# An LSTM with a sign-weight FFN on one core: Wx in two pieces, twelve steps' x products ahead, and FFN weights made from step 4

## The chip, the core and the metric

The kernel runs on one NeuronCore of a Trainium2 chip. The time is that of the device for one execution, in microseconds (us); the kernel before has three such runs. A profiled execution, taken by the hardware profiler, is a fourth one: its trace gives every duration below.

Five engines work beside each other, each with its own queue of instructions: TensorE (PE: matrix products; its weight loads are the row PEld), VectorE (DVE), ScalarE (ACT), GpSimd (POOL) and SyncE (SP, which here only issues DMA requests). ACT and POOL issue DMA requests too. Matrix products accumulate in PSUM; everything else lies in SBUF, 128 partitions wide.

## What is computed

The input x has N=32 sequences of T=64 steps with D=256 features. An LSTM with H=256 runs over it, and its outputs go through three layers whose weights are boolean matrices read as +1 and -1:

```python
def lstm_forward(x, h0, Wx, Wh, b):
    xW = jnp.einsum('ntd,dg->ntg', x, Wx) + b
    def step(carry, xw_t):
        prev_h, prev_c = carry
        a = xw_t + prev_h @ Wh            # 4 gates of 256
        i, f, o = sigmoid(a[:, :Hd]), sigmoid(a[:, Hd:2*Hd]), sigmoid(a[:, 2*Hd:3*Hd])
        g = jnp.tanh(a[:, 3*Hd:])
        next_c = f * prev_c + i * g
        next_h = o * jnp.tanh(next_c)
        return ((next_h, next_c), next_h)
...
h = jnp.concatenate([hs, -hs], axis=-1)
h = relu(s0 * conn_dense(k0, h)) * 2      # 512 -> 1024, conn_dense: w = where(k, 1.0, -1.0)
h = relu(s1 * conn_dense(k1, h)) * 2      # 1024 -> 1024
out = x + s2 * conn_dense(k2, h)          # 1024 -> 256
```

The 64 steps of the LSTM depend on each other; the products of x with Wx and the FFN don't depend on the next step.

## The kernel before

**Layout.** The four quarters (`NQ = 4`) of the 256 features lie in the four groups of 32 partitions; in a product each quarter is a matmul of its own with 32 columns of weights. A product in full f32 is two matmul instructions in the trace. The gates lie in the order of `GATES`: slot 0 is the candidate (tanh), slots 1 and 2 are the sigmoid gates i and f, slot 3 is o.

**Loads (L116-139, L143-146, L430-433).** SP and ACT issue them in the order of the program: the first four steps of x, slots 2 and 3 of Wx (128 KB a request, four requests), x of steps 4 to 7, slots 0 and 1 of Wx, x of steps 8 to 15, then Wh (slot 0, then slots 1 to 3). From there SP alone goes on: x of steps 16 to 31 (L138, L139), the eight requests for k0 (L146), four rows of k1 (L182), x of steps 32 to 47 (L433). ACT has an activation of its own between its requests (L120), which brings in its table of functions. POOL loads the bias, the first h and the scales. The tile framework gives these requests a set of semaphores in turn, so a later request waits until an earlier one has landed.

**Before step 0 (L422-450).** PE runs two matmuls on zeros into the gate banks and `WARM_UP` = 9 more into an idle bank. Then come the products of x with Wx for steps 0 to 7: first slots 2 and 3 of all eight steps (for each step both contraction chunks k), then slots 0 and 1, and after each pair of steps `evict_x` (L238), in which DVE adds the bias and moves two steps to SBUF as `xg`. `x_products(8, AHEAD)` with `AHEAD` = 10 does steps 8 and 9 with all four slots. `turn_x` (L210) is the DVE transpose of half a block of x (eight steps) that these products read.

**The steps (L467-482).** In step t the program issues, in this order:

- `gates_from_h` (L265): 32 matmul instructions, h times Wh, on top of what lies in the two gate banks;
- `cell_step` (L283): on ACT two sigmoids and a tanh, on DVE `kept`, `new`, `c`, on ACT `th`, on DVE `h` and its transpose into `hist`; then ACT copies `xg` of the next step into the gate banks (L280, L281);
- one **chore** from a list of 16, one a step from step 0 on (L458-461, L470): four pieces of w0 (`make_w0`, L186: an ACT instruction on the spot, L189, and a DVE one later in the step, L190), eight rows of w1 (`make_w1`, L194: one ACT instruction of 1024 columns, and the load of another row), four pieces of w2 (`make_w2`, L198);
- work for PE: in steps 0 to 20 (`X_STEPS` = 21) a 21st of the x products that are left, after that a share of the FFN (`ffn_block`, L365). In units of `x_part` (L222; 8 matmul instructions, one step and one chunk of all slots) that is five units in most steps and six in three;
- the DVE half of a w0 chore, and every fourth step `split_h` (L308), which makes the FFN's two-part input (`hhi` on ACT, `hlo` on DVE).

After each pair of steps, `x_products` calls `evict_x`; where the half block after is to be turned (L253-257), it calls `turn_x` and asks for the half block four further on.

After step 63 the last FFN block runs by itself (L484).

Of the kernel before, what the change touches and what calls it, by code (L numbers as in the profile page):

```python
# [32 lines left out]
AF = mybir.ActivationFunctionType  # L33
# [5 lines left out]
def lstm_ffn(ctx: ExitStack, tc: tile.TileContext, x, cond, wx_d, wh_d, b_d, k0_d, k1_d, k2_d, s0_d, s1_d, s2_d, out):  # L39
    nc = tc.nc  # L40
    P = 128
    N, T, D = x.shape
    H = cond.shape[1]
# [6 lines left out]
    SB = 16  # L50
    NB = T // SB
# [2 lines left out]

    GATES = (3, 0, 1, 2)

    AHEAD = 10
    X_STEPS = 21
    WARM_UP = 9

    const = ctx.enter_context(tc.tile_pool(name="const", bufs=1))
    xpool = ctx.enter_context(tc.tile_pool(name="x", bufs=4))
# [10 lines left out]
    def act(shape, dtype, name):  # L73
        return apool.tile(shape, dtype, tag="act", name=name)
# [4 lines left out]
    def load_x(i, half, engines, part=slice(0, SB // 2)):  # L79
        if part.start == 0:  # L80
            xq[i, half] = xpool.tile([P, SB // 2, HQ], F32, tag="x", name=f"x{i}_{half}")
        t0 = i * SB + half * (SB // 2)
        for q in range(NQ):
            engines[q % len(engines)].dma_start(  # L84
                out=xq[i, half][q * N : (q + 1) * N, part],
                in_=x[:, t0 + part.start : t0 + part.stop, ts(q, HQ)],
            )
# [6 lines left out]
    wx = const.tile([P, 2, G], F32, name="wx")  # L94
# [4 lines left out]
    warm = const.tile([P, 40], F32, name="warm")  # L99
# [4 lines left out]
    def rows(t, q):  # L104
        return t[q * 32 : (q + 1) * 32]

    def load_gates(t, w_d, slots, engines):

        w_rows = w_d.rearrange("(q b j) g -> q j b g", q=NQ, b=2)
        s0, n, g0 = slots[0], len(slots), GATES[slots[0]]  # L110
        for q in range(NQ):
            engines[q % len(engines)].dma_start(
                out=rows(t, q)[:, :, s0 * H : (s0 + n) * H], in_=w_rows[q, :, :, g0 * H : (g0 + n) * H]
            )

    load_x(0, 0, [nc.sync, nc.scalar], slice(0, SB // 4))  # L116
    load_gates(wx, wx_d, (2, 3), [nc.sync, nc.scalar])
    load_x(0, 0, [nc.sync, nc.scalar], slice(SB // 4, SB // 2))

    nc.scalar.activation(warm[:, 1:2], warm[:, :1], AF.Sigmoid)  # L120

    b_rows = b_d.rearrange("(g q j) -> q g j", g=4, q=NQ)
    for q in range(NQ):
# [2 lines left out]
    for slot in range(2):  # L126
        load_gates(wx, wx_d, (slot,), [nc.sync, nc.scalar])
    load_x(0, 1, [nc.sync, nc.scalar])
    load_gates(wh, wh_d, (0,), [nc.sync, nc.scalar])
    load_gates(wh, wh_d, (1, 2, 3), [nc.sync, nc.scalar])  # L130
    h_first = const.tile([P, HQ], F32, name="h_first")
    nc.gpsimd.dma_start(out=h_first, in_=cond.rearrange("n (q j) -> q n j", q=NQ))
    scales = []
# [9 lines left out]
    for i in range(2):  # L143
        t = act([P, 2, F0], U8, f"k0_{i}")
# [65 lines left out]
    def turn_x(i, half, part=slice(0, SB // 2)):  # L210
        if part.start == 0:
            xT[i, half] = act([P, SB // 2, 2, N], F32, f"xT{i}_{half}")
        nc.vector.transpose(
            xT[i, half][:, part].rearrange("p t b n -> p (t b n)"),
            xq[i, half][:, part].rearrange("p t j -> p (t j)"),
        )
# [5 lines left out]
    def x_part(p, t, k, slots, start):  # L222

        i, s = divmod(t, SB // 2)
        for q in range(NQ):
            nc.tensor.matmul(  # L226
                p[q * N : (q + 1) * N, t % 2, slots],
                xT[i // 2, i % 2][:, s, k, :],
                wx_q[:, k, q, slots],
                start=start,  # L230
                stop=False,
                skip_group_check=True,
            )

    def x_bank(t):
        return ps_f.tile([P, 2, 4, HQ], F32, tag="pf", name=f"px{t}")

    def evict_x(p, t):  # L238
        xg[t] = gpool.tile([P, 2, 4 * HQ], F32, tag="xg", name=f"xg{t}")
        b = bias[:, :4].rearrange("p g j -> p (g j)").unsqueeze(1).to_broadcast([P, 2, 4 * HQ])  # L240
        nc.vector.tensor_tensor(xg[t], p.rearrange("p t g j -> p t (g j)"), b, ALU.add)  # L241

    def x_products(t0, t1):

        for t in range(t0, t1, 2):
            p = x_bank(t)
            for s in range(2):
                for k in range(2):
                    x_part(p, t + s, k, slice(0, 4), s == 0 and k == 0)
                    if s == 1 and k == 1:  # L250
                        evict_x(p, t)

                        half, left = divmod(t + 2, SB // 2)  # L253
                        if left == SB // 4 and half + 1 < 2 * NB:
                            turn_x(*divmod(half + 1, 2))
                            if half + 5 < 2 * NB:
                                load_x(*divmod(half + 5, 2), [nc.sync])
                    yield 2


# [4 lines left out]
    def gates_from_h(t, hT):  # L265
        for g, slots in zip(gates, (slice(0, 3), slice(3, 4))):
            for k in range(2):
                for q in range(NQ):
                    nc.tensor.matmul(  # L269
                        g[q * N : (q + 1) * N],  # L270
                        hT[:, k, :],
                        wh_q[:, k, q, slots],
                        start=False,
                        stop=(k == 1),
                        skip_group_check=True,
                    )
# [6 lines left out]
    def cell_step(t, c):  # L283
        sig = cell.tile([P, 3, HQ], F32, tag="sig", name=f"sig{t}")
        cand = cell.tile([P, HQ], F32, tag="cand", name=f"cand{t}")
        nc.scalar.activation(sig[:, 0:2, :], gates[0][:, 1:3], AF.Sigmoid)  # L286
        nc.scalar.activation(cand, gates[0][:, 0], AF.Tanh)  # L287
        nc.scalar.activation(sig[:, 2, :], gates[1][:, 0], AF.Sigmoid)  # L288
        kept = cell.tile([P, HQ], F32, tag="kept", name=f"kept{t}")
        nc.vector.tensor_mul(kept, sig[:, 1, :], c)  # L290
        new = cell.tile([P, HQ], F32, tag="new", name=f"new{t}")
        nc.vector.tensor_mul(new, sig[:, 0, :], cand)  # L292
        c = cell.tile([P, HQ], F32, tag="c", name=f"c{t}")
        nc.vector.tensor_add(c, kept, new)  # L294
        th = cell.tile([P, HQ], F32, tag="th", name=f"th{t}")
        nc.scalar.activation(th, c, AF.Tanh)  # L296
        h = cell.tile([P, HQ], F32, tag="h", name=f"h{t}")
        nc.vector.tensor_mul(h, sig[:, 2, :], th)  # L298
        i, s = divmod(t, SH)
        if s == 0:  # L300
            hist[i] = hpool.tile([P, 2, SH * N], F32, tag="hist", name=f"hist{i}")
        hT = hist[i][:, :, ts(s, N)]
        nc.vector.transpose(hT, h.rearrange("p (b j) -> p b j", b=2))  # L303
        if t + 1 < T:
            gates_from_x(t + 1)
        return c, hT
# [116 lines left out]
    for g in gates:  # L423
        g = g.rearrange("p g j -> p (g j)")
        nc.tensor.matmul(g, idle[:, :P], idle[:, : g.shape[1]], start=True, stop=True)
    for n in range(WARM_UP):
        nc.tensor.matmul(p_idle, idle[:, :P], idle, start=True, stop=True)
# [8 lines left out]
    nc.vector.memset(c, 0.0)  # L436

    banks = [x_bank(t) for t in range(0, SB // 2, 2)]
    for slots in (slice(2, 4), slice(0, 2)):
        for t in range(SB // 2):  # L440
            for k in range(2):
                x_part(banks[t // 2], t, k, slots, slots.start == 2 and t % 2 == 0 and k == 0)
            if slots.start == 0 and t % 2:
                evict_x(banks[t // 2], t - 1)
            if slots.start == 0 and t == 1:
                turn_x(0, 1)
    nc.vector.transpose(hT, h_first.rearrange("p (b j) -> p b j", b=2))
    for _ in x_products(SB // 2, AHEAD):
        pass
# [3 lines left out]
    def ffn():  # L453
        for b in range(NB):
            yield from ffn_block(b)


    chores = deque()  # L458
    chores += [lambda k=k, h=h: make_w0(k, h) for k in range(2) for h in range(2)]
    chores += [lambda k=k: make_w1(k) for k in range(FC0)]  # L460
    chores += [lambda k=k, m=m: make_w2(k, m) for k in range(2) for m in range(2)]

    work = x_products(AHEAD, T)
    total_x = (T - AHEAD) * 4
    total_ffn = (NB - 1) * (4 * FC0 + 2 * FC0 * FC1 + 4 * FC1)
    done = 0
    for t in range(T):  # L467
        gates_from_h(t, hT)
        c, hT = cell_step(t, c)
        later = chores.popleft()() if chores else None  # L470
        if outputs and next(outputs[0], "end") == "end":
            outputs.popleft()
        if t == X_STEPS:
            work, done = ffn(), 0
        goal = (t + 1) * total_x // X_STEPS if t < X_STEPS else (t + 1 - X_STEPS) * total_ffn // (T - X_STEPS)
        while done < goal:
            done += next(work)
        if t == X_STEPS - 1:
            next(work, None)
        if callable(later):  # L480
            later()
        if t % SH == SH - 1:
            split_h(t // SH)
# [31 lines left out]
```

## Time and profile before

| What | Value |
|---|---|
| Three runs | 323.43, 323.81, 324.02 us; median 323.81 us |
| Profiled execution, its own time | 325.26 us |
| Its span, first to last instruction | 323.5 us |
| PE busy with matmuls | 309.4 us (96% of the span) |
| DVE, ACT, POOL busy | 154.0, 131.0, 9.2 us |
| Mean granted TensorE clock | 0.991 |
| First product of x | 6.85 us |
| First matmul of step 0, of step 21 | 17.57 us, 89.48 us |

Times in the trace count from the start of the span. In lists of instructions the columns are start, duration, engine, line, operation, output and inputs, how often, and in brackets the idle time just before it on its engine with what ended it. Rows of merged instructions give the stretch from the first one's start to the last one's end. A busy PE is one with matmuls in flight, which need not mean that it runs at its full rate.

### The profile page before, as it was taken

The page shows a single profiled execution, that of the slowest core. Times are in us where ns is not written, and L with a number is a line of the kernel's source. Part 1 is how long each engine was busy: PE and PEld are TensorE (multiplying, and loading weights), DVE is VectorE, ACT ScalarE, POOL GpSimd, SP SyncE. Part 2 cuts the span into 40 slices and gives each one's busy share as a digit, 9 for nine tenths or more (in the row PEclk, how much of TensorE's full clock was granted, in tenths as well). Part 3 has the DMA queues.
Part 4 walks back from the last instruction along what each step waited for, and adds up shares of the span by engine and source line. Part 5 has one row for each costly group of instructions (what it writes and reads, how often), then busy time and mean ns, then how long its engine had stood idle before and what let it go on. Part 6 is the DMA issues. An engine that isn't in the chain of part 4 may idle for free.

```text
span 323.5 us, 9433 instructions
## 1 busy us (share of the span) xinstructions
PE 309.4 (96%) x3979; PEld 236.8 (73%) x3979; DVE 154.0 (48%) x473; ACT 131.0 (41%) x484; POOL 9.2 (3%) x28
## 2 busy tenths in 40 slices
PE   6994999999999999999999999999999999999992
PEld 3963677787777777777777777777777777888881
DVE  1345765767576433334855433457453333811113
ACT  1015578754455434334735333455433432511111
POOL 3500000000000000000000000000000000000001
PEclk9997999999999999999999999999999999999998
DMA  6745321311000000000010100000310000230002
GB/s 147 208 101 149 71 57 35 86 34 35 6 2 2 0 2 2 1 2 2 0 35 2 32 3 2 2 0 9 92 32 4 2 0 2 58 72 2 0 0 65
DMA packets 30937, 10.99 MB, mean 34 GB/s; under 512 B 28008, under 2 KB 30312, under 8 KB 30896
## 3 DMA queue, kind: packets, MB, share of 16 engines
q1 hardware_dynamic: 27616, 8.66, 11.1%
q10 hardware_dynamic: 3008, 1.57, 1.9%
q8 instruction: 31, 0.51, 0.7%
q0 software_dynamic: 272, 0.17, 0.3%
q14 instruction: 10, 0.08, 0.1%
HBM read 8.29 MB, written 2.10 MB: 32 GB/s over the span
## 4 chain that ended last, share of the span: by engine, by line
PE 87%; DMA 5%; DVE 3%; SPq 3%; issue 1%; ACT 1%; DVEq 0%; ACTq 0%
PE p L399 38%; PE gates L269 19%; PE px L226 12%; PE p L371 10%; PE po L384 9%; DMA x<-in_x_dram 2%; DMA wh<-in_L_cond_Wh_dram 2%; SPq L146 1%; SPq L84 1%; DMA k<-in_L_ffn_k_dram 1%; DMA wx<-in_L_cond_Wx_dram 1%; DVE w L190 0%; DVE xg L241 0%; ACT th L296 0%; DVE hist L303 0%
## 5 line engine op out<-in xcount | busy, mean ns | idle before, releaser
L269 PEld LDWEIGHTS gates<-wh,hist 128*32 128x32 f32 x2016 | 54.6, 110 | 30.3 <-issue 14.1
L269 PE MATMUL gates<-wh,hist 128*32 128x192 f32 x2016 | 68.9, 277 | 5.0 <-DVE hist L303 5.0
L226 PE MATMUL px<-wx,xT 128*32 128x256 f32 (+1 forms) x1152 | 62.2, 366 | 1.4 <-DMA wx<-in_L_cond_Wx_dram 1.4
L226 PEld LDWEIGHTS px<-wx,xT 128*32 128x32 f32 x1152 | 41.3, 115 | 13.8 <-issue 2.7
L286 ACT ACTIVATE sig<-gates 128x128 f32<-128x128 f32 x64 | 17.7, 277 | 82.7 <-PE gates L269 82.5
L290 DVE TENSOR_TENSOR kept<-sig,c 128x64 f32<-128x64 f32 x63 | 14.1, 224 | 61.1 <-ACT sig L286 60.9
L296 ACT ACTIVATE th<-c 128x64 f32<-128x64 f32 x64 | 16.4, 257 | 32.0 <-DVE c L294 32.0
L371 PE MATMUL p<-hhi,w 128*128 128x512 f32 x64 | 25.5, 399 | 0.0
L371 PE MATMUL p<-hlo,w 128*128 128x512 f32 x64 | 25.3, 395 | 0.0
L298 DVE TENSOR_TENSOR h<-sig,th 128x64 f32<-128x64 f32 x64 | 14.4, 226 | 20.7 <-ACT th L296 20.7
L241 DVE TENSOR_TENSOR xg<-px,bias 128x512 f32<-128x512 f32 x32 | 21.2, 666 | 5.9 <-POOL nsgn L158 4.8
L280 ACT COPY gates<-xg 128x192 f32<-128x192 f32 x64 | 20.0, 313 | 8.4 <-DVE xg L241 8.4
L303 DVE STREAM_TRANSPOSE hist<-h 128x64 f32<-128x64 f32 x64 | 15.7, 245 | 2.4
L294 DVE TENSOR_TENSOR c<-kept,new 128x64 f32<-128x64 f32 x64 | 14.4, 225 | 2.2
L288 ACT ACTIVATE sig<-gates 128x64 f32<-128x64 f32 x64 | 14.8, 231 | 0.0
L371 PEld LDWEIGHTS p<-hhi,w 128*128 128x128 f32 x64 | 12.0, 188 | 2.8
L287 ACT ACTIVATE cand<-gates 128x64 f32<-128x64 f32 x64 | 14.0, 218 | 0.1
L292 DVE TENSOR_TENSOR new<-sig,cand 128x64 f32<-128x64 f32 x64 | 13.9, 218 | 0.0
L371 PEld LDWEIGHTS p<-hlo,w 128*128 128x128 f32 x64 | 12.0, 188 | 2.6
L399 PE MATMUL p<-a_7h,w 128*128 128x512 f32 x32 | 13.0, 407 | 0.0
L281 ACT COPY gates<-xg 128x64 f32<-128x64 f32 x64 | 13.0, 203 | 0.0
L399 PE MATMUL p<-a_2l,w 128*128 128x512 f32 x32 | 12.9, 403 | 0.0
(121 smaller groups left out, 500.5 us busy)
## 6 DMA issues: line engine op xcount, KB each, us to landing
x<-in_x_dram SPq DMA_DIRECT2D x58, 64.0 KB, 2.4
out_dram<-o SPq DMA_DIRECT2D x28, 64.0 KB, 1.8
bits<-in_L_ffn_k_dram SPq DMA_DIRECT2D x10, 128.0 KB, 2.5
k<-in_L_ffn_k_dram SPq DMA_DIRECT2D x8, 64.0 KB, 2.0
wh<-in_L_cond_Wh_dram SPq DMA_DIRECT2D x2, 192.0 KB, 5.3
wh<-in_L_cond_Wh_dram ACTq DMA_DIRECT2D x2, 192.0 KB, 5.1
wx<-in_L_cond_Wx_dram SPq DMA_DIRECT2D x2, 128.0 KB, 3.5
wx<-in_L_cond_Wx_dram ACTq DMA_DIRECT2D x2, 128.0 KB, 4.1
```

The lines of the kernel that those rows point to most:

```text
L226: nc.tensor.matmul(p[q * N : (q + 1) * N, t % 2, slots], xT[i // 2, i % 2][:, s, k, :], wx_q[:, k, q, slots], start=start, stop=False, ski ...
L241: nc.vector.tensor_tensor(xg[t], p.rearrange("p t g j -> p t (g j)"), b, ALU.add)
L269: nc.tensor.matmul(g[q * N : (q + 1) * N], hT[:, k, :], wh_q[:, k, q, slots], start=False, stop=(k == 1), skip_group_check=True,)
L280: nc.scalar.copy(gates[0], x_t[:, :3])
L286: nc.scalar.activation(sig[:, 0:2, :], gates[0][:, 1:3], AF.Sigmoid)
L288: nc.scalar.activation(sig[:, 2, :], gates[1][:, 0], AF.Sigmoid)
L294: nc.vector.tensor_add(c, kept, new)
L296: nc.scalar.activation(th, c, AF.Tanh)
L303: nc.vector.transpose(hT, h.rearrange("p (b j) -> p b j", b=2))
L371: nc.tensor.matmul(p, w0[:, k, ts(m, P)], a[:, k, :], start=(n == 0), stop=(n == 3))
L384: nc.tensor.matmul(po[m], w2[:, m, k], a1[k][n], start=(k == 0 and n == 0), stop=(k == FC1 - 1 and n == 1))
L399: nc.tensor.matmul(p1[m], w1[:, k, ts(m, P)], a0[k][n], start=(k == 0 and n == 0), stop=(k == FC0 - 1 and n == 1),)
```

## The change

- Slots 2 and 3 of Wx are loaded in two pieces, chunk 0 of the contraction and then chunk 1: eight requests of 64 KB in place of four of 128 KB. The x of steps 4 to 7 is requested after them.
- The first products go by chunk: chunk 0 of steps 0 to 3, chunk 1 of steps 0 to 3, then the same of steps 4 to 7. Slots 0 and 1 go as before.
- `AHEAD` is 12: steps 8 to 11 are multiplied ahead of step 0, and two steps fewer are left for steps 0 to 20.
- The turn of x of steps 16 to 23, which would fall at the end of the part ahead, is called in step 0 behind `cell_step` (`next_x`), with the load that belongs to it.
- The chores start at step 4 (`FIRST_CHORE`), so they end with step 19 and not with step 15.
- `WARM_UP` is 8, and ACT's first activation, with its table load, stands behind its last load request.

```diff
-    AHEAD = 10
+    AHEAD = 12
     X_STEPS = 21
-    WARM_UP = 9
+
+    FIRST_CHORE = 4
+    WARM_UP = 8
...
-    def load_gates(t, w_d, slots, engines):
+    def load_gates(t, w_d, slots, engines, chunks=slice(0, 2)):
...
-                out=rows(t, q)[:, :, s0 * H : (s0 + n) * H], in_=w_rows[q, :, :, g0 * H : (g0 + n) * H]
+                out=rows(t, q)[:, chunks, s0 * H : (s0 + n) * H],
+                in_=w_rows[q, :, chunks, g0 * H : (g0 + n) * H],
...
     load_x(0, 0, [nc.sync, nc.scalar], slice(0, SB // 4))
-    load_gates(wx, wx_d, (2, 3), [nc.sync, nc.scalar])
+    for k in range(2):
+        load_gates(wx, wx_d, (2, 3), [nc.sync, nc.scalar], slice(k, k + 1))
     load_x(0, 0, [nc.sync, nc.scalar], slice(SB // 4, SB // 2))
-
-    nc.scalar.activation(warm[:, 1:2], warm[:, :1], AF.Sigmoid)
...
     load_gates(wh, wh_d, (1, 2, 3), [nc.sync, nc.scalar])
+
+    nc.scalar.activation(warm[:, 1:2], warm[:, :1], AF.Sigmoid)
...
+    def next_x(half):
+
+        if half < 2 * NB:
+            turn_x(*divmod(half, 2))
+            if half + 4 < 2 * NB:
+                load_x(*divmod(half + 4, 2), [nc.sync])
...
-                        if left == SB // 4 and half + 1 < 2 * NB:
-                            turn_x(*divmod(half + 1, 2))
-                            if half + 5 < 2 * NB:
-                                load_x(*divmod(half + 5, 2), [nc.sync])
+                        if left == SB // 4 and t + 2 != AHEAD:
+                            next_x(half + 1)
...
-    for slots in (slice(2, 4), slice(0, 2)):
-        for t in range(SB // 2):
-            for k in range(2):
-                x_part(banks[t // 2], t, k, slots, slots.start == 2 and t % 2 == 0 and k == 0)
-            if slots.start == 0 and t % 2:
-                evict_x(banks[t // 2], t - 1)
-            if slots.start == 0 and t == 1:
-                turn_x(0, 1)
+    late, early = slice(0, 2), slice(2, 4)
+    for k, t in [(k, t) for t0 in (0, SB // 4) for k in range(2) for t in range(t0, t0 + SB // 4)]:
+        x_part(banks[t // 2], t, k, early, t % 2 == 0 and k == 0)
+    for t in range(SB // 2):
+        for k in range(2):
+            x_part(banks[t // 2], t, k, late, False)
+        if t % 2:
+            evict_x(banks[t // 2], t - 1)
+        if t == 1:
+            turn_x(0, 1)
...
-        later = chores.popleft()() if chores else None
+        if t == 0:
+            next_x(AHEAD // (SB // 2) + 1)
+        later = chores.popleft()() if t >= FIRST_CHORE and chores else None
```

## The prediction

> **What bounds the kernel now.** I read the page first, then PE's instructions in order of time, then the stretch in which PE is idle, engine by engine, and last the loads.
>
> ```profile
> PE 309.4 (96%) x3979; PEld 236.8 (73%) x3979; DVE 154.0 (48%) x473; ACT 131.0 (41%) x484; POOL 9.2 (3%) x28
> ...
> L269 PE MATMUL gates<-wh,hist 128*32 128x192 f32 x2016 | 68.9, 277 | 5.0 <-DVE hist L303 5.0
> L226 PE MATMUL px<-wx,xT 128*32 128x256 f32 (+1 forms) x1152 | 62.2, 366 | 1.4 <-DMA wx<-in_L_cond_Wx_dram 1.4
> ```
>
> PE is the bound at 96%, and its idle time has few places: 5.0 us before gate products, 1.4 us before the first product of x, and the ends. PE in order of time, steps 0 to 2:
>
> ```profile
> 17.57 1.08 PE L269 MATMUL gates<-wh,hT_first 128*32 128x192 f32 x32
> 18.44 2.37 PE L226 MATMUL px<-wx,xT 128*32 128x256 f32 x40
> 20.59 1.08 PE L269 MATMUL gates<-wh,hist 128*32 128x192 f32 x32
> 21.47 2.37 PE L226 MATMUL px<-wx,xT 128*32 128x256 f32 x40
> 28.50 1.93 PE L269 MATMUL gates<-wh,hist 128*32 128x192 f32 x32 [4.67 <-DVE hist L303]
> ```
>
> I write G0, G1 ... for the start of each step's gate products. G1-G0 is 3.03 us (20.59-17.57; unrounded starts), as in most later steps; G2 comes 7.91 us after G1. The same stretch on all engines says why:
>
> ```profile
> 19.10 5.47 SPq L146 DMA_DIRECT2D k<-in_L_ffn_k_dram  x8
> ...
> 24.34 0.72 ACT L189 ACTIVATE w0t<-k,sgn 128x512 f32<-128x512 uint8 x1 [4.22 <-DMA k<-in_L_ffn_k_dram]
> ...
> 24.97 0.26 ACT L286 ACTIVATE sig<-gates 128x128 f32<-128x128 f32 x1
> ...
> 26.25 0.75 DVE L190 SCALAR_TENSOR_TENSOR w<-k,nsgn,w0t 128x512 fp32r<-128x512 uint8 x1 [4.51 <-DMA k<-in_L_ffn_k_dram]
> ```
>
> Step 0's chore reads k0, whose requests SP issues from 19.10 and whose last lands at 26.13. Step 1's sigmoids are queued behind it on ACT, its `kept` behind L190 on DVE, and PE's step 2 behind those. The stretches of one microsecond after it show a second price (PEclk is the figure before the DMA share):
>
> ```profile
> 26.00:27.00 1.00, 0.00 (x0) 0.00 (x0) 0.75 (x2) 0.00 (x0) 0.00 (x0) 1.00 0.82 256
> ...
> 28.00:29.00 1.00, 0.49 (x8) 0.43 (x12) 0.97 (x4) 0.84 (x3) 0.00 (x0) 0.50 0.82 206
> 29.00:30.00 1.00, 1.00 (x25) 0.71 (x20) 0.62 (x1) 0.00 (x0) 0.00 (x0) 0.50 0.69 155
> ```
>
> The clock is halved from 27.75 to 31.17, and G3-G2 is 4.33 us. The start is slow too: the same product form, first in 7 to 10 us, then in 11 to 15 us.
>
> ```profile
> L226 PE MATMUL px<-wx,xT x60: 392/418/421, 6.9 to 9.9; 128*32 128x128 f32 x60
> ...
> L226 PE MATMUL px<-wx,xT x156: 272/273/273, 10.8 to 15.0; 128*32 128x128 f32 x156
> ```
>
> Groups of four start every 213 ns until 10.69, every 107 ns after it. The clock row doesn't show this: its first record is the rise at 10.69.
>
> [...] 3.41 us at half clock, and rises at 10.69 and 31.17. Whether matmuls on zeros count as activity isn't settled: the window up to 3.86 was some 77% busy with them and brought no rise, that up to 31.17 was 78% busy with real ones and did. [...] SP's and ACT's requests here also took at least 1.84 us. [...]
>
> **The change, part by part.** The sum is made against the profiled execution, 325.26 us (span 323.5, 1.8 us around it).
>
> *Chores from step 4.* Step 1 goes from 7.91 to 3.03: -4.88 us. With the idle stretch the halved clock goes: step 2 from 4.33 to 3.03, -1.30. At step 4, G0+4·3.03+2.73 = about 32.4 for ACT and DVE, k0 (26.13) has been there for 6 us. What is late next in steps 0 to 3 is PE itself: a step's chain, gates to `hist`, is 2.73 us and the next gates can start 0.15 later (39.76 to 39.90), so 2.88, against PE's 3.03.
>
> But the w0 chores were partly covered by the stall, and now meet full steps on DVE. What such a meeting costs is seen at the end of step 3, on DVE in order of time:
>
> ```profile
> 35.48 1.33 DVE L241 TENSOR_TENSOR xg<-px,bias 128x512 f32<-128x512 f32 x2
> 36.72 0.70 DVE L213 STREAM_TRANSPOSE xT<-x 128x512 f32<-128x512 f32 x1
> 37.35 0.71 DVE L190 SCALAR_TENSOR_TENSOR w<-k,nsgn,w0t 128x512 fp32r<-128x512 uint8 x1
> 37.98 0.42 DVE L319 TENSOR_TENSOR hlo<-hist,hhi 128x256 fp32r<-128x256 f32 x1
> 38.31 0.22 DVE L290 TENSOR_TENSOR kept<-sig,c 128x64 f32<-128x64 f32 x1
> ```
>
> `kept` at 38.31 is 2.01 after G4 (36.30), where 1.27 is usual: 0.74 late, and G5-G4 is 3.60, 0.57 over. That goes. In its place: x units are 5 a step, an eviction follows every eighth. Step 4 (units 21 to 25; 24 evicts): eviction at +2.86 from its G, 0.69, w0 0.75, done at 4.30, just when the next `kept` is due (3.03+1.27): nothing. Step 6 (unit 32, and the turn): from `hist` at 2.73, 0.69+0.70+0.75 = 4.87: 0.57 late, less 0.15 slack, 0.42 lost. Step 7 (unit 40 at its end, and `hlo`): from 3.29, 0.69+0.75+0.42 = 5.15: 0.85 late, 0.70 lost. Together +1.12, bounds 0.4 and 1.8. The w1 and w2 chores did their work in running steps before too (all their steps together are 0.24 us over): I keep that.
>
> *Twelve steps ahead.* Two steps of x are 8 units of 8 instructions. A five-unit step adds 40 in 2.16 us, so 54 ns each; -0.43 us for each unit taken out of a step. Before: 18 steps of five, three of six, 18·3.03+3·3.46 = 64.92. After: 104 units, 20 steps of five and one of four, and that one is bound by its chain: 20·3.03+2.88 = 63.48. So -1.44. The eight units taken out of those steps and the first two pairs lie before G0.
>
> *G0.* It needs two things. **Wh**: its last request left ACT at 12.48 and landed at 17.43; G0 followed 0.14 later. From the ninth request on, each goes out as the one eight before it lands (7.03 after 7.01, 8.64 after 8.63). With four more requests Wh's last quarter still hangs on the landing of x for steps 8 to 15, whose chain goes through the second Wx pieces in place of the whole ones. Those end with the same 512 KB, at about 6.6; ACT, which sent requests without a break from 7.37 to 9.65, can send earlier ones. I put Wh at 16.5 to 17.4. **PE**: the 128 KB requests landed at 4.67, 5.45, 6.05, 6.60; half the bytes are in by about 5.2, so the first product starts at 5.45 instead of 6.85 (+0.25 as before). The eight warm-up matmuls end at 5.05 (5.48-0.43). Chunk 0 of four steps is 32 instructions, 1.7 us at half rate: chunk 1, in at 6.7, isn't waited for; x of steps 4 to 7, which leaves after chunk 0 has landed and so lands near 7.6, is turned by 8.1, before PE wants it at 8.9. The work: 256·26.7 ns + 64·54 ns = 10.29 us at full rate, 0.24 of small gaps (from the same sum for before), and half the cold time. Cold until 7.27, the next window's end: 16.9. Cold until 10.69 as now: 18.6. So G0 is 17.0 to 18.6, now 17.57. I take no gain and no loss; the 1.7 us more work is what the earlier start pays for.
>
> *Table load.* 1.28 us on ACT, now after its last request (about 12), done before the copies into the gate banks (14.12 now) or a little after, with G0 3 us off: nothing. Without that cover it would delay G0 by 1.28. Before, ACT's next request waited for a landing at 6.60 anyway, so nothing is won there. *next_x in step 0*: the turn (0.70) stands on DVE at G0+2.73 = 20.3, ahead of step 1's `kept`; its x landed at 18.69 and may come 2 us later before anyone waits. Its load on SP stands behind requests that are sent by 33.65, and the next k1 row is asked for in step 8: nothing.
>
> **Sum**: -4.88 -1.30 -0.57 +1.12 -1.44 +0 = -7.07: 318.2 us on the profiled execution. The median of the runs is 1.45 lower. If that is the profiler's share, the median after is 316.7. If it is the halved clock (1.30), [...] there is that much less to gain: 318.0. I take 317.4.
>
> **Rivals.**
> - *Earlier start, full rate at once*: zeros count as activity, Wh lands at 16.7, G0 16.8 (-0.8), and DVE's meetings cost 0.5 less: 316.1. For it: gap of 0.4 us in place of 1.4 in the window up to 7.27. Against: no rise at 3.86.
> - *Cold start*: zeros don't count, G0 18.6 (+1.0) and the meetings cost 0.5 more: 318.9.
> - *The stall returns at step 4*, because k0 comes 12 us later than now: SP's queue would have to slip. What is left is -1.44 -0.57 +1.12: 322.9. Nothing in the trace speaks for it.
> - *Slower*: the new order makes PE wait for piece after piece, so that [...] all the work ahead runs at half rate: 5.45+2·10.29 = 26.0 for G0, 8.5 later, 325.9. It decides from G0 about 24. Against it: at half rate PE has 1.7 us for each piece, longer than pieces are apart.
>
> **How the numbers follow.** Forecast 0.60 (own range 316.5 to 318.4), earlier start 0.17, cold start 0.17, stall returns 0.02, slower 0.04. The range, 315.4 to 319.3, takes in the first three with their bounds. Within 0.2% (0.65 us, about what a measurement of this kernel can tell from no change) 0.01, half of the returning stall; slower 0.04; faster 0.95.
>
> **What would show it.** First product at 5.3 to 5.6; no wait of L189 on k0; G2-G1 and G3-G2 3.03; no halved clock between 20 and 300 us; G21-G0 64.8 instead of 71.91, with steps 6 and 7 the long ones; G0 between 17.0 and 18.6. I am wrong if PE has a new idle stretch over 1 us before step 21, or if the steps from 21 on (unchanged) take other than their 4.2 us or so.

## The result, and the profile after

The changed kernel takes 319.17 us (median of four runs, 318.56 to 319.47) against 323.62 us: ratio 0.9862, 95% interval 0.9839 to 0.9885. Its profiled execution took 319.36 us, its span is 317.6 us; against the profiled execution before, 5.9 us less.

The page after, the lines that answer to those of before (the code has moved: gates are L277, x products L230):

```profile
PE 306.2 (96%) x3978; PEld 235.5 (74%) x3978; DVE 153.7 (48%) x473; ACT 130.7 (41%) x484; POOL 9.1 (3%) x28
...
L277 PE MATMUL gates<-wh,hist 128*32 128x192 f32 x2016 | 68.1, 275 | 0.4 <-DVE hist L311 0.3
L230 PE MATMUL px<-wx,xT 128*32 128x256 f32 (+1 forms) x1152 | 60.6, 356 | 3.7 <-DMA wh<-in_L_cond_Wh_dram 2.6
```

The 5.0 us before gate products have gone to 0.4. But the 1.4 us before the products of x have become 3.7. PE in order of time shows both; first the steps:

```profile
19.51 1.08 PE L277 MATMUL gates<-wh,hT_first 128*32 128x192 f32 x32
20.38 2.37 PE L230 MATMUL px<-wx,xT 128*32 128x256 f32 x40
22.54 1.08 PE L277 MATMUL gates<-wh,hist 128*32 128x192 f32 x32
23.41 2.37 PE L230 MATMUL px<-wx,xT 128*32 128x256 f32 x40
25.57 1.08 PE L277 MATMUL gates<-wh,hist 128*32 128x192 f32 x32
```

G1-G0, G2-G1 and G3-G2 are 3.03. The first chore, in ACT's and DVE's own order, waits for nothing (no bracket behind it):

```profile
34.55 0.72 ACT L193 ACTIVATE w0t<-k,sgn 128x512 f32<-128x512 uint8 x1
35.36 0.75 DVE L194 SCALAR_TENSOR_TENSOR w<-k,nsgn,w0t 128x512 fp32r<-128x512 uint8 x1
```

The stretches in which the clock had been halved (PEclk before the DMA share):

```profile
24.00:28.00 4.00, 4.00 (x99) 3.12 (x92) 2.24 (x10) 1.64 (x10) 0.00 (x0) 1.00 0.74 198
28.00:32.00 4.00, 4.00 (x98) 3.22 (x94) 2.57 (x10) 1.65 (x8) 0.00 (x0) 1.00 0.40 89
```

Then the part ahead of step 0:

```profile
1.45 3.31 PE L435 MATMUL p_idle<-idle 128*128 128x512 bf16 x8
5.36 1.08 PE L230 MATMUL px<-wx,xT 128*32 128x128 f32 x32 [0.60 <-DMA wx<-in_L_cond_Wx_dram]
6.77 3.17 PE L230 MATMUL px<-wx,xT 128*32 128x128 f32 x96 [0.33 <-DMA wx<-in_L_cond_Wx_dram]
12.57 7.16 PE L230 MATMUL px<-wx,xT 128*32 128x128 f32 x192 [2.63 <-DMA wh<-in_L_cond_Wh_dram]
```

PE begins at 5.36, at full rate (granted clock 1.00 from 4.32 on), and stands from 9.94 to 12.57. The row blames Wh, but products of x don't read Wh. By the landings it is the last request for slot 1 of Wx (12.32). In the eleven profiles in which slot 1 is left for these late products (those of slots 0 and 1), they begin 0.05 to 0.35 us after its landing, or PE comes to them later and doesn't wait for it. G0 is 19.51, against 17.57.

So the 5.9 us of the two profiled executions are: G0 +1.94, G21-G0 from 71.91 to 64.41 (-7.50), the rest -0.32. Each of these is one execution; how far G0 moves between executions of the same code is taken up in experiment 3.

### The profile page after: what moved, and what is told of

It reads as the page before. It is cut to its first block, busy times and chain, and to the rows that moved or that the text cites. A ratio compares the mean times of both kernels' runs of the same rounds, so it can differ in the third digit from the quotient of the medians.

```text
span 317.6 us, 9440 instructions
## 1 busy us (share of the span) xinstructions
PE 306.2 (96%) x3978; PEld 235.5 (74%) x3978; DVE 153.7 (48%) x473; ACT 130.7 (41%) x484; POOL 9.1 (3%) x28
## 4 chain that ended last, share of the span: by engine, by line
PE 91%; DMA 3%; DVE 3%; issue 1%; ACT 1%; ACTq 0%; DVEq 0%
PE p L407 38%; PE gates L277 19%; PE px L230 14%; PE p L379 10%; PE po L392 9%; DMA wx<-in_L_cond_Wx_dram 2%; DMA wh<-in_L_cond_Wh_dram 1%; DMA x<-in_x_dram 1%; DVE xg L245 1%; DVE w L194 0%; ACT th L304 0%; DVE c L302 0%; DVE h L306 0%; DVE o L362 0%; ACTq L86 0%
## 5 line engine op out<-in xcount | busy, mean ns | idle before, releaser
L277 PEld LDWEIGHTS gates<-wh,hist 128*32 128x32 f32 x2016 | 54.5, 110 | 25.2 <-issue 14.1
L277 PE MATMUL gates<-wh,hist 128*32 128x192 f32 x2016 | 68.1, 275 | 0.4 <-DVE hist L311 0.3
L230 PE MATMUL px<-wx,xT 128*32 128x256 f32 (+1 forms) x1152 | 60.6, 356 | 3.7 <-DMA wh<-in_L_cond_Wh_dram 2.6
L230 PEld LDWEIGHTS px<-wx,xT 128*32 128x32 f32 x1152 | 40.0, 110 | 15.4 <-DMA x<-in_x_dram 2.9
```

The lines of the kernel that those rows point to most:

```text
L230: nc.tensor.matmul(p[q * N : (q + 1) * N, t % 2, slots], xT[i // 2, i % 2][:, s, k, :], wx_q[:, k, q, slots], start=start, stop=False, ski ...
L277: nc.tensor.matmul(g[q * N : (q + 1) * N], hT[:, k, :], wh_q[:, k, q, slots], start=False, stop=(k == 1), skip_group_check=True,)
```

## The experiments

All ratios are against the kernel before, with 95% intervals. The times in the traces are those of one profiled execution each.

**1. The chores alone.** The kernel before with

```diff
-        later = chores.popleft()() if chores else None
+        later = chores.popleft()() if t >= 4 and chores else None
```

> The kernel before with one edit: chores from step 4 on. Theory (the stall of step 1 is the whole gain, and what the change does ahead of step 0 costs about as much as the two steps taken out of the loop bring): G0 stays at 17.6, G2-G1 and G3-G2 are 3.03, and the time is 4.7 us below the kernel before, up to 6.0 where the halved clock had been in its runs: 317.7 to 319.0, as low as the whole change (319.2) or lower. Rival (the parts ahead of step 0 bring 1.5 us or more of the 4.5): 320.7 or more.

Measured: 319.45 us, ratio 0.9866 (0.9826 to 0.9906), so as low as the whole change. PE in order of time:

```profile
6.59 3.71 PE L226 MATMUL px<-wx,xT 128*32 128x128 f32 x128 [1.45 <-DMA wx<-in_L_cond_Wx_dram]
11.00 5.43 PE L226 MATMUL px<-wx,xT 128*32 128x128 f32 x160 [0.70 <-DMA x<-in_x_dram]
18.31 1.08 PE L269 MATMUL gates<-wh,hT_first 128*32 128x192 f32 x32 [1.89 <-DMA wh<-in_L_cond_Wh_dram]
...
21.34 1.08 PE L269 MATMUL gates<-wh,hist 128*32 128x192 f32 x32
```

The steps behave as forecast (G2-G1 and G3-G2 3.03, G21-G0 65.64). G0 is 18.31 and not 17.6: here the clock rose at 4.66, not at 10.68, PE was at full rate from its first product of x, was through early, and waited 1.89 us for Wh. The edit doesn't touch that part of the program. So in this load order, too, the loads hold G0, and a faster PE ahead of it gained nothing.

**2. Everything but the chores.** The changed kernel with `FIRST_CHORE = 0`.

```diff
-    FIRST_CHORE = 4
+    FIRST_CHORE = 0
```

> The changed kernel with the chores from step 0 again, all else as changed. Theory (the stall is a wait for k0, whose landing doesn't move with G0): k0 lands at 25.6 as in the changed kernel, step 2 begins at 27.9 or so, 5.4 after step 1 instead of 3.03, so 2.4 us more; the meetings on DVE in steps 4 and 7 (0.76) go in part: 1.7 to 2.4 us over the changed kernel, 321 to 321.6. Rival (the stall has its own length, 4.9 us and a halved clock): 324 or more.

Measured: 324.3 us, ratio 1.0016 (0.9994 to 1.0038): all the gain is gone. My expectation was wrong. PE in order of time:

```profile
18.09 1.08 PE L277 MATMUL gates<-wh,hT_first 128*32 128x192 f32 x32
...
21.12 1.08 PE L277 MATMUL gates<-wh,hist 128*32 128x192 f32 x32
...
28.85 1.93 PE L277 MATMUL gates<-wh,hist 128*32 128x192 f32 x32 [4.50 <-DVE hist L311]
```

I had held G0 at 19.5 and k0's landing at 25.6; they were 18.09 and 26.48, the wait was 4.50, and the clock was halved from 28.74 to 32.16. The time is the one that the rival named, but its reason, a stall of fixed length, doesn't hold: G2-G1 is 7.74 here and 7.91 and 6.25 in the two profiles of the kernel before (the second is experiment 4). What stays the same is the distance from k0's last landing to step 2, 2.37 us in all three (28.85-26.48, 28.50-26.13, 27.26-24.89). So what is won ahead of step 0 can't show while the stall stands. The units taken out of the later steps do show behind it: G21-G2 is 59.99 here, 60.98 and 61.38 in the kernel before. But k0 landed 0.35 and 1.59 us later here than there, which took part of it back or all of it; why it did isn't shown. Without the stall the other parts bring no more than can be measured (experiment 1).

**3. Chores from step 2.** The changed kernel with

```diff
-    FIRST_CHORE = 4
+    FIRST_CHORE = 2
```

> The changed kernel with chores from step 2 instead of 4. Theory (the stall is a wait for k0, which lands at 25 to 26.5; step 2's chore comes up on ACT at 28): no wait of the first chore, G2-G1 and G3-G2 3.03, the meetings on DVE fall into other steps with 0.3 to 1.2 us in all: within 0.5 us of the changed kernel, 318.7 to 319.7. Rival (from step 0 to step 4 each step that the chores come sooner costs its share of the 4.5 us): 321 or more.

Measured: 318.63 us, ratio 0.9821 (0.9787 to 0.9855). The first chore starts on ACT at 27.43, behind k0 (26.19), without a wait; G2-G1 and G3-G2 are 3.03. So it is a threshold, not a share for each step. The meeting on DVE moved into step 4: G5-G4 is 3.96. It is the lowest median of all kernels here, but its interval overlaps that of the changed kernel.

The edits of this experiment and of experiment 2 leave everything ahead of step 0 as in the changed kernel. Yet the late products and G0 came at other times, first in experiment 2, then in this one:

```profile
11.10 7.15 PE L230 MATMUL px<-wx,xT 128*32 128x128 f32 x192 [1.03 <-DMA x<-in_x_dram]
...
10.78 7.15 PE L230 MATMUL px<-wx,xT 128*32 128x128 f32 x192 [0.80 <-DMA x<-in_x_dram]
18.88 1.08 PE L277 MATMUL gates<-wh,hT_first 128*32 128x192 f32 x32 [0.94 <-DMA x<-in_x_dram]
```

(By the landings the first waits are again for slot 1 of Wx, 10.86 and 10.54, and the last is for Wh, 18.47.) So G0 was 19.51, 18.09 and 18.88 for one and the same code ahead of it; for that of the kernel before it was 17.57, 17.98 (experiment 4) and 18.31 (experiment 1). A G0 from one profile can be off by more than a microsecond, and the differences of G0 in the experiments below aren't shown to be effects of their edits.

**4. The kernel before once more**, unchanged, for a second profiled execution.

> The kernel before, unchanged, profiled once more. Theory (the profiled execution was 1.45 us above its median because the halved clock after the stall fell into it, and it need not fall into every one): if the clock isn't halved in steps 2 and 3 here, G3-G2 is 3.0 to 3.1 and the profiled time is near the median; if it is, 4.3 again and a time above the median. Rival (the 1.45 us are the profiler's own): the profiled time is 1.4 above the median with or without the halved clock.

Measured: 323.83 us, ratio 0.999 (0.9969 to 1.0012). The profiled execution took 324.31, half a microsecond above its median, with a shorter stall:

```profile
21.01 1.08 PE L269 MATMUL gates<-wh,hist 128*32 128x192 f32 x32
...
27.26 1.16 PE L269 MATMUL gates<-wh,hist 128*32 128x192 f32 x32 [3.01 <-DVE hist L303]
28.13 4.05 PE L226 MATMUL px<-wx,xT 128*32 128x256 f32 x40
31.97 1.08 PE L269 MATMUL gates<-wh,hist 128*32 128x192 f32 x32
```

G2-G1 is 6.25 and G3-G2 4.71 (7.91 and 4.33 in the first), the clock halved again. On this chip, 43 runs of the kernel before went from 321.86 to 326.58. So my first profiled execution, 325.26, was one of its long ones. The theory, that the halved clock made it long and need not fall into every execution, is borne out in part. It need not: of the 63 runs on this chip (43, and 20 of this experiment) nine had a mean granted clock of 0.997 or 0.998, which by my estimate leaves room for 2.3 us at half clock (at most 0.35% of 322 us, twice), less than the 3.41 us of the halved stretch in the first profile. They took 322.04 to 323.52, median 322.71, some 1.1 us under the median of all. Five had 0.983 and took 325.38 to 326.58. (A longer stall could also bring more halving; the times alone don't part the two.) But 44 of the 63 had 0.992 or less, more than the 1.3 to 4.2 us of halved clock at the end of every profile here can account for, and so has the median: the clock was halved in all three profiles with the stall, also in one near its median (experiment 2). Against this second profile the first is 1.0 us longer with one halved stretch in each: in the first, k0 landed 1.24 us later (26.13, 24.89 here). The profiler's own share is small: the changed kernel's profiled time lies 0.2 above its median.

**5. Wx in whole requests.** The changed kernel, its products still by chunk, with

```diff
-    for k in range(2):
-        load_gates(wx, wx_d, (2, 3), [nc.sync, nc.scalar], slice(k, k + 1))
+    load_gates(wx, wx_d, (2, 3), [nc.sync, nc.scalar])
```

> The changed kernel with slots 2 and 3 of Wx in whole requests again (four of 128 KB), the order of the products left by chunk. Theory (slot 1 of Wx lands late because PE's own instruction fetch, [...] goes out when PE is through the early products): PE starts at 6.8 at full rate, is through at 10.3, the fetch still falls on the last requests of slot 1, they land after 11.8, G0 is 19.0 to 19.5, time 318.7 to 319.4. Rival (the four more requests push slot 1 back): it lands by 10.9 as in the kernel before, G0 17.7, time about 317.4.

Measured: 318.97 us, ratio 0.9846 (0.9816 to 0.9877), the same as the changed kernel within the interval. Slot 1 landed by 10.26, as the rival said; the fetch (the 16 KB packet that the DMA view lists as "instruction"; that it is PE's is my reading, more on it below) went out at 10.33, behind it. But the clock fell back to half from 7.34 to 10.75, after PE had stood from 4.6 to 6.64, so PE was the slow one, without a wait, and G0 came to 18.74. Neither forecast of G0 was met.

**6. A longer warm-up.** `WARM_UP` 20 instead of 8.

```diff
-    WARM_UP = 8
+    WARM_UP = 20
```

> The changed kernel with 20 matmuls on zeros in place of 8: 2.6 us of useless work ahead of the first product. Theory (fetch): early products end at 10.8, the fetch goes out after the last of Wx has landed (10.5 or so), PE doesn't wait at the late products, G0 17.8 to 18.3, time 317.5 to 318.0, faster for doing more. Rivals (more requests; or a DMA rate that gives the data no sooner): slot 1 still lands at 12.3, G0 19.5, time 319.2.

Measured: 319.19 us, ratio 0.9852 (0.9822 to 0.9882). PE didn't begin before 8.61, since the clock rose only at 7.02 here; slot 1 had landed at 11.49, before the fetch at 11.61, and PE didn't wait for it. Then Wh came at 19.55 and G0 at 19.96. Not faster and not slower: both expectations of G0 missed.

**7. Many small warm-up products.**

```diff
         nc.tensor.matmul(p_idle, idle[:, :P], idle, start=True, stop=True)
+    for n in range(48):
+        nc.tensor.matmul(p_idle[:32, :128], idle[:, :32], idle[:, :128], start=True, stop=True)
```

> The changed kernel with 48 small matmuls on zeros (32 columns of weights, 128 moving) behind the 8: about the same 2.6 us of PE time as twelve large ones, but 72 more instructions, [...]. Theory (fetch): it falls on the last requests of slot 1 again, they land after 11.5, G0 18.8 to 19.5, time 318.5 to 319.3. Rival (what counts is only when PE begins): as with twelve large ones, whatever those give.

Measured: 319.54 us, ratio 0.9858 (0.9828 to 0.9889). The fetch went out at 10.55, sooner than with twelve large ones (11.61); that the number of instructions decides this was my estimate, and isn't shown. Slot 1 landed at 11.40, G0 was 19.65. Landing, G0 and time all lie outside what the fetch theory forecast (after 11.5, 18.8 to 19.5, 318.5 to 319.3), though not by much. The last of slot 1's sixteen parts came only 0.22 us behind the others, so nothing here shows that the fetch held it up. Experiment 6 gave no faster kernel to set against this one, so the pair doesn't tell.

**8. Three slots of Wx in the early pieces.** The changed kernel with

```diff
-        load_gates(wx, wx_d, (2, 3), [nc.sync, nc.scalar], slice(k, k + 1))
+        load_gates(wx, wx_d, (1, 2, 3), [nc.sync, nc.scalar], slice(k, k + 1))
...
-    for slot in range(2):
-        load_gates(wx, wx_d, (slot,), [nc.sync, nc.scalar])
+    load_gates(wx, wx_d, (0,), [nc.sync, nc.scalar])
...
-    late, early = slice(0, 2), slice(2, 4)
+    late, early = slice(0, 1), slice(1, 4)
```

> The changed kernel with three slots of Wx (1, 2 and 3) in the two early pieces and slot 0 alone left for the late products. Theory (PE's wait before the late products, 9.7 to 12.6, is the loss ahead of step 0): the early products now take 5.1 us instead of 3.4, so PE is busy until the last of Wx has landed (10.5 to 12.3), the wait falls under 0.6 us, and G0 is set by Wh at 17.9 to 18.3 instead of 19.5: 317.6 to 318.0. Rival (Wh is what holds G0, or the first piece comes so much later that nothing is won): G0 19.2 or more, 318.9 to 319.5.

Measured: 318.9 us, ratio 0.9849 (0.9807 to 0.989). PE in order of time:

```profile
6.33 1.51 PE L229 MATMUL px<-wx,xT 128*32 128x192 f32 x32 [1.31 <-DMA wx<-in_L_cond_Wx_dram]
8.47 5.29 PE L229 MATMUL px<-wx,xT 128*32 128x192 f32 x178 [0.63 <-DMA wx<-in_L_cond_Wx_dram]
14.57 4.32 PE L229 MATMUL px<-wx,xT 128*32 128x64 f32 x110 [0.81 <-issue]
18.62 1.08 PE L276 MATMUL gates<-wh,hT_first 128*32 128x192 f32 x29
```

The wait for slot 1 is gone, G0 is 0.9 sooner, the span 0.6 shorter; G0 lies within what the changed kernel's own code gave (18.09 to 19.51). In the wait's place stand 0.6 us for the second piece and 0.81 us in which PE waits for nothing that the profile shows. The median's gain is within the interval.

**9. Three slots and 14 steps ahead**: the edits of experiment 8, and the x products ended a step earlier.

```diff
-    AHEAD = 12
-    X_STEPS = 21
+    AHEAD = 14
+    X_STEPS = 20
...
-                        if left == SB // 4 and t + 2 != AHEAD:
+                        if left == SB // 4 and t + 2 != 12:
```

> As the three-slot kernel, with 14 steps ahead, and the x products ended in step 19 instead of 20 (the FFN begins a step earlier). Theory: 1.7 us more PE work ahead of step 0 where PE would wait for Wh, so G0 18.6 to 19.0, and four units fewer in the loop, -1.73: 316.7 to 317.3. Rival (the work ahead isn't covered by a wait and only moves): as the three-slot kernel, within 0.5.

Measured: 320.22 us, ratio 0.9889 (0.9851 to 0.9927), more than expected by 3 us. G0 was 19.67, and G1-G0 4.01: the products of step 16 came up in step 0, before their x was turned (PE waits 0.71 us for it). Other meetings on DVE cost 0.3 to 0.4 in steps 8, 12 and 16.

**10. Ten steps ahead.** The changed kernel with

```diff
-    AHEAD = 12
+    AHEAD = 10
...
-        if t == 0:
-            next_x(AHEAD // (SB // 2) + 1)
```

> The changed kernel with 10 steps ahead instead of 12 (the turn of x for step 16 back in its old place). Theory (work ahead is worth something only where PE would wait for Wh): PE is through 1.73 us sooner, G0 follows Wh at 18.0 to 18.5, 1.0 to 1.5 sooner, and four units more in the loop cost 1.44: within 0.5 us of the changed kernel. Rival (each unit ahead is a unit saved, G0 is set by Wh or by slot 1 alone): G0 near 19.5 and 1.4 us more, 320.6.

Measured: 321.27 us, ratio 0.9906 (0.9871 to 0.9941); the interval overlaps the changed kernel's a little. PE in order of time:

```profile
13.10 5.43 PE L230 MATMUL px<-wx,xT 128*32 128x128 f32 x160 [3.04 <-DMA wh<-in_L_cond_Wh_dram]
19.11 1.08 PE L277 MATMUL gates<-wh,hT_first 128*32 128x192 f32 x32 [0.59 <-DMA x<-in_x_dram]
```

G21-G0 is 65.77, 1.36 more, against 1.44 forecast for four units. But G0 came only 0.40 sooner, since Wh landed at 18.66 (the row names x, the landings say Wh). So in this execution most of the work of steps 10 and 11 lay in a wait for Wh, and twelve steps bring about 1 us between the two profiled executions. As G0 moves by that much by itself, this is a size, not a measured gain.

**11. The table load back between ACT's requests.**

```diff
     load_x(0, 0, [nc.sync, nc.scalar], slice(SB // 4, SB // 2))
+
+    nc.scalar.activation(warm[:, 1:2], warm[:, :1], AF.Sigmoid)
...
-    nc.scalar.activation(warm[:, 1:2], warm[:, :1], AF.Sigmoid)
     h_first = const.tile([P, HQ], F32, name="h_first")
```

> The changed kernel with ACT's table load back between its requests, behind the x of steps 4 to 7. Theory (ACT's requests for slots 0 and 1 of Wx are on the path to G0): ACT is held to 6.9, its requests of slot 1 leave 0.5 to 0.9 later, the late products begin 0.3 to 0.9 later, G0 19.6 to 20.4, 319.4 to 320.1. Rival (as forecast, nothing: the requests wait for landings anyway): within 0.2 of the changed kernel, 319.0 to 319.4.

Measured: 319.51 us, ratio 0.9863 (0.9826 to 0.9901). The median falls into the theory's range, but neither G0 (19.18) nor the late products (from 12.06, sooner than in the changed kernel) came later, as it needs: nothing that can be measured.

**12. Three slots and chores from step 2**: the edits of experiments 8 and 3.

> The three-slot kernel with chores from step 2, the candidate for the fastest. Theory: G0 as with three slots (18.1 to 18.7, against 19.5 in the changed kernel), the steps as with chores from step 2: 318.0 to 318.8. Rival (G0 gains nothing that can be measured): 318.9 to 319.4.

Measured: 319.15 us, ratio 0.9839 (0.9806 to 0.9871). G0 was 18.38, but G5-G4 went to 4.11 (3.30 in the changed kernel, 3.96 in experiment 3, so it comes with the chores from step 2). No kernel here beats the changed one by more than the intervals.

## Why the prediction was right, and where it wasn't

The direction, the cause and the range were right: the gain is the chore's wait for k0 and what it drags behind it. Experiments 1 and 2 show it from both sides: 0.9866 with that edit alone, 1.0016 without it. The forecast of 317.4 was 1.8 us too low, and the terms say why. One of the prediction's own signs of being wrong did appear, a new idle stretch of PE over 1 us before step 21: 2.63 us, ahead of step 0.

| Term | Forecast | Measured |
|---|---|---|
| Step 1 | 7.91 to 3.03 | 3.03 |
| Step 2, halved clock | 4.33 to 3.03 | 3.03, no halved clock |
| G21-G0 | 64.8 | 64.41 |
| Over the count of units (63.48) | 1.36 | 0.93 |
| First product | 5.45 | 5.36 |
| Last landing of Wh | 16.5 to 17.4 | 18.14 |
| G0 | 17.57, bounds 17.0 and 18.6 | 19.51 (18.09 and 18.88 in experiments 2 and 3) |
| From G21 to the end | unchanged | 0.32 less |

**G0 is the step that failed.** The prediction let it need two things, Wh and PE's work. It put Wh too early: 18.14, and 17.59 and 18.47 in the other two profiles of this code, against 16.5 to 17.4. (The least time of a request that it names, 1.84 us, is about that of the loads, 1.83 in that trace; stores of the output took 1.63 there. The estimate of Wh doesn't rest on that.) And it left out a third thing: slots 0 and 1 of Wx, which the late products read. At half rate, as before, PE came to them at about 12.2, after they had landed (10.88), and no row showed a wait. (That slow start was itself a matter of one execution: in experiments 1 and 4, with the same code, the clock rose at 4.66 and 4.23, and the late products did wait, 0.70 and 0.51 us.) In the changed kernel the clock rose at 4.32, when PE had run nothing but the warm-up on zeros, the early products took 3.4 us of work and were through at 9.94, and PE stood until 12.57. What is left then is 128 instructions of 26.7 ns and 64 of 54 ns, 6.9 us: 19.5. I had taken the earlier start and the full rate for gains, up to 0.8 us in the early rival. They are none, because the data comes no sooner: over the fourteen profiles here Wh landed between 17.4 and 19.6, and G0 lay between 17.6 and 20.0, never ahead of Wh. The loss of 1.94 us is that of two single executions; the means over three profiles of each code, 17.95 and 18.83, are 0.9 apart.

Why slot 1 came so late is shown in part. The sixteen parts in which its last request lands, from the trace of the changed kernel:

```
10.10 10.26 10.37 10.54 10.55 10.67 10.69 10.74 10.77 10.79 10.83 10.84 10.85 10.94 10.95 12.32
```

Fifteen are in by 10.95; one, which PE needs as much as the others, is 1.37 us late. The DMA queues in the stretch from 10 to 11 us (queue, packets, MB, share of sixteen engines) have a guest:

```profile
q10 hardware_dynamic: 259, 0.07, 28.8%
q1 hardware_dynamic: 246, 0.06, 28.0%
q8 instruction: 1, 0.02, 6.2%
```

One packet of 16 KB, listed as "instruction", begins at 10.24 and takes 0.98 us (6.2% of sixteen engines' time in this microsecond is one engine for 0.99 us). Its time moves with PE's progress (9.24 to 11.98 in the profiles), so I take it for a fetch of PE's instructions, and the late part for that of the engine which carried it. Neither is shown: the trace doesn't name the engines. But over the profiles the packet and the late part go together. I took, from the fetch on, the first request of which one part came over 0.6 us behind the other fifteen. In thirteen of the fourteen profiles that part landed 1.08 to 1.29 us after the fetch packet had ended, wherever that was (10.56 to 12.91); before it, from 7.5 us on, no part was more than 0.53 us behind. In the fourteenth, experiment 7, a part was 0.50 us behind, 1.41 us after the packet. So slot 1 was hit in three of the seven profiles with pieces of two slots, by 0.81 to 1.53 us (the changed kernel, experiments 10 and 11), and not in experiments 2 and 3, where the same code ahead of step 0 had it in by 10.86 and 10.54. That a part falls behind after the fetch is thus shown by its timing; that the fetch keeps one engine back, and that it is PE's fetch, fits this but stays argued.

The other part is the pieces. In the four profiles with whole requests slot 1 had landed by 10.26 to 10.88, in the seven with pieces of two slots by 10.54 to 12.77. Here a request went out only when the one eight before it had landed (in the changed kernel Wh's at 11.21 and 12.35, after landings at 11.20 and 12.32), so smaller requests leave fewer bytes in flight: by 8 us, the packets begun on the queues of SP and ACT came to 1010 to 1046 KB in the four with whole requests and to 903 to 990 KB in the seven with pieces. (The three profiles with pieces of three slots, 96 KB a request, had 1054 to 1082 KB.) No experiment kept the fetch away and let all else stand, so the shares stay open.

**The meetings on DVE** were sized near enough (0.93 for all, forecast 1.36), but in wrong places, because of a slip. Two steps of x are four units, not eight as I wrote; the totals, 108 and 104, and the sums from them were right, but evictions follow every fourth unit. So step 4's chore met nothing, and what I laid into steps 6 and 7 came as 0.27 at the end of step 3, with a turn and no chore, and 0.49 at the end of step 7. There DVE in order of time has, after the change:

```profile
43.81 1.25 DVE L245 TENSOR_TENSOR xg<-px,bias 128x512 f32<-128x512 f32 x2
44.98 0.73 DVE L194 SCALAR_TENSOR_TENSOR w<-k,nsgn,w0t 128x512 fp32r<-128x512 uint8 x1
45.63 0.42 DVE L327 TENSOR_TENSOR hlo<-hist,hhi 128x256 fp32r<-128x256 f32 x1
45.97 0.22 DVE L298 TENSOR_TENSOR kept<-sig,c 128x64 f32<-128x64 f32 x1
```

`kept` is 1.94 behind G8 (44.03) instead of 1.27.

**Table load: nothing**, right within the interval of experiment 11, some 1.2 us to either side. **Chunk 1 isn't waited for**: wrong by 0.33 us, since PE was at full rate. **The base of the sum**: the profiled execution before was a long one. Against the median the change is -4.5, against that execution -5.9. On the profiled execution the sum said 318.2 and 319.36 came: 1.94 lost at G0, 0.4 less in steps 0 to 20, 0.3 less after them. The other 0.6 of the miss is the middle of 316.7 and 318.0, which was a guess about the difference between that execution and the median. The 319.17 us lie 0.1 under the upper end of the range, which stood there for a cold start; G0 came late for another reason, so it is in part luck that the range held.

**The rivals.** The clock did rise behind zeros alone (at 4.32), as the early start had it, but its gain didn't come. The stall didn't return, and PE wasn't slow ahead of step 0.

## What to carry to other kernels

In the kernel before, step 1's sigmoid stood ready for 3.3 us (its gates were done at 21.67) and came only behind the chore on ACT (24.34, then 24.97). So a small operation can cost what its data is late, for everything that is queued behind it on its engine; ask first whether it can stand a few steps later, and look for the step from which its data is there. While such a stall stands, what is won ahead of it vanishes in it, so undo the parts one at a time, from both ends. Before work is started earlier, list every load that it reads, also those that show no wait today: a faster engine can meet the ones that a slow engine had hidden (here slot 1 of Wx: no wait in the kernel before's first profile, 2.63 us in the changed kernel). And profile the kernel twice before its first microseconds are put into a sum: the second profile of this one would have shown the early clock and the wait that the first one hid.

## What the runs showed that I had not expected

- The profile lists packets of 16 KB under the kind "instruction" among the DMA traffic (q8: 31 packets, 0.51 MB, 0.6% of sixteen engines in the changed kernel), and they may come in the way twice: after one of them, one part of a load lands late (12.32 against 10.95 in the changed kernel), and perhaps they come late themselves. In experiment 8 the fetch went out at 11.94, and PE later stood 0.81 us for "issue"; in the same kernel with chores from step 2 it went out at 11.34, and PE stood 0.81 us again. That the two belong together isn't shown.
- The clock rose when PE had run nothing but matmuls on zeros: at 4.32 in the changed kernel, a microsecond ahead of its first real product (5.36). The changes of the clock within the profile of the kernel before lie whole multiples of 3.41 us apart (10.68, 27.75 and 31.16: 17.07 is five times 3.41). The windows of the forecast, and those here, are stretches of 3.41 us counted back from such a change: an estimate, since no record marks them. The window up to 3.86 in the kernel before was 77% busy with zeros and the clock didn't rise; the one up to 3.92 in experiment 5 was 79% busy, and it rose. In that kernel, the next window was about 40% busy, and the clock fell back (7.34). In the second profile of the kernel before, with the same code as the first, the window ended at 4.23, was 88% busy, and the clock rose. So the same code can start at full or at half rate (rise at 10.68, or at 4.23); that this hangs on where the windows fall is my estimate, and what share of a window decides isn't shown.
- The stalled kernel's time goes with its mean granted clock. It scatters over 4.7 us in 43 runs (321.86 to 326.58), with the clock between 0.998 and 0.983, and the five runs at 0.983 lie between 325.38 and 326.58 (experiment 4). The four runs of the changed kernel lie within 0.9 us, at 0.996 to 0.998, but four are few: of the twelve runs of experiments 1 and 11, which have no stall either, nine at 0.995 or more took 318.76 to 320.55, and three at 0.990 to 0.992 took 321.35 to 321.75.
